# Layer 0 of a four-layer graph network on one NeuronCore: one strided sum per chunk in place of adding halves

## The chip, the core and the metric

The kernel runs on one core of one Trainium2 chip. The metric is the device time of one execution in microseconds; the time before is the median of three timed runs. One more execution was recorded by the hardware profiler. The engines are named as the profile names them: PE (TensorE's matmuls; PEld are its weight loads), DVE (VectorE), ACT (ScalarE), POOL (GpSimd) and SP (SyncE). In this kernel POOL issues the gathers and scatters through index lists (DMA_INDIRECT), and SP issues the plain DMAs.

## The reference

Four layers of message passing over the same graph: 3125 nodes with 128 features, 100000 edges sorted by destination. Each layer ends in a residual and a layer norm. Only layer 0 is touched by the change:

```python
z_bar = segment_sum(z[edge_type], dst) / max(deg, 1)
pre_self = h @ P1 + h @ P2 + z_bar @ P3
pre_edge = (h @ P1)[dst] + (h @ P2)[src] + (z @ P3)[edge_type]
logit_self, logit_edge = leaky(pre_self) @ y_w, leaky(pre_edge) @ y_w
alpha = softmax over a node's edges and its self edge        # 8 heads
t_self = h @ Wh + z_bar @ Wz
t_edge = (h @ Wh)[src] + (z @ Wz)[edge_type]
agg = segment_sum(alpha * t, dst)                            # 8 heads of 16
out = leaky(agg + residual_weight * h)                       # h itself where deg is 0
```

Layers 1 to 3 are a mean aggregation with a two-layer MLP, an attention with edge biases, and an attention with node and edge types.

## The kernel before

Nodes are ordered by degree and cut into 25 tiles of 128 (NT), one node per partition. A tile's edges stand in slots: tile t has CAP[t] of them, from 57 down to 21, 821 in all. Slots are worked in chunks of at most W = 8, so 114 chunks, 92 of them full. A loop for nodes of higher degree (`behind`, with `behind0` as its body) runs zero times on this input, so its gathers and sums are in the code and not in the trace.

For each chunk of layer 0, POOL gathers per slot one row of h_tab by source node into `hs` (264 numbers per slot: 128 for the logits, 128 for the message, 8 for the self logits). The edge's share by type comes in one of two ways:

- `gathered` (67 chunks, 45 of them full): POOL gathers per slot one row of z_tab into `zs` (328 numbers per slot: 264 that are added to hs, at L808, and 64 of z itself). The sum of the 64 over the slots is added to `za` (a part of the tile `az`), at L810.
- `multiplied` (47 chunks, all full): the edge types are made into one-hot matrices on VectorE (L834), and PE forms z transposed, `zT` (128 x 1024), from them. PE then forms the additions to hs (L849), which VectorE adds (L850). The sum of zT over the slots is kept in `zbT`.

Then PE transposes hs or multiplies it with the identity (L815, L843), VectorE adds the node's own term (L787), ACT applies a relu (L788), and PE forms the logits (L790). When all chunks of a tile are there, `masked` and `softmax` run, and `spread` (L872 to L874) multiplies each chunk's messages in hs by the weights in place, sums them over the slots, and adds the sum to `ac`, the other part of `az`.

`halved` makes these three kinds of sum: it adds the second half of the slots to the first (L796) until two are left, and adds those (L799). For 8 slots that is an add over 4 slots, one over 2 and one over 1. It works in place in hs and zs, and in `zh` for zT, whose first add is L853. The last reader of a chunk's `hs` is L874, and that of a chunk's `zs` is L810.

Buffers: hs has 8, so a gather into hs waits until the chunk eight places earlier has been spread. zs, zT and zh have 2 each.

Between the chunks a second job is interleaved step by step: `counts` builds, for layer 1, the matrix of edge counts from one-hot matrices (L562 to L639: c_oh, c_oha, c_ohb, c_ohs, c_ohd on VectorE, c_perm and c_ps on PE, c_sb on ACT, c_tab to DRAM by SP). At a tile's end the self edge, the norm and layer 1's first product follow (L929 to L988). For the next tile `prologue` gathers x (L772) one tile ahead.

The order of instructions on each engine is not the order of the source: a scheduler lays out each engine's queue ahead of the run, and each engine then works through its queue strictly in that order. So the same source lines can stand in another order when an instruction near them changes. Layers 2 and 3 do the weighted sum over slots in `weigh` (L696 to L701).

Of the kernel before, what the change touches and what calls it, by code (L numbers as in the profile page):

```python
# [8 lines left out]
F32 = mybir.dt.float32  # L9
# [4 lines left out]
OP = mybir.AluOpType  # L14
AX = mybir.AxisListType
# [3 lines left out]
P = 128  # L19
# [8 lines left out]
W = 8  # L28
D = 128
# [5 lines left out]
R = 64  # L35
HC = 2 * D + H
# [39 lines left out]
def tile_gnn(ctx, tc, a, out):  # L76
    nc = tc.nc
    V, A, G, T = nc.vector, nc.scalar, nc.gpsimd, nc.tensor
# [10 lines left out]
    def gather(dst, table, idx, **kw):  # L89
        return G.indirect_dma_start(out=dst, out_offset=None, in_=table, in_offset=indirect(idx), **kw)  # L90
# [394 lines left out]
    with tc.tile_pool(name="srcp", bufs=1) as sp, tc.tile_pool(name="srcq", bufs=2, space=PSUM) as ps:  # L485
# [28 lines left out]
        for o in range(0, NS, P):  # L514
            n = min(P, NS - o)
# [232 lines left out]
    with tc.tile_pool(name="l0", bufs=2) as wp, tc.tile_pool(name="l0s", bufs=1) as sp, \  # L748
# [14 lines left out]
        def sums_of(t):  # L763
            az = wp.tile([P, D + R], F32, name="az")
            nc.sync.dma_start(az, sums_at[t])
            return az[:, :D], az[:, D:], az
# [17 lines left out]
        def logits(pre, k, h1T, lg_ps):  # L784

            low = wp.tile([P, 4, P], F32, name="low")
            V.tensor_add(low[:, :k], pre[:, :k], h1T.unsqueeze(1).to_broadcast([P, k, P]))  # L787
            A.activation(low[:, :k], low[:, :k], AF.Relu)  # L788
            for s in range(k):
                T.matmul(lg_ps[:, s, :], low[:, s, :], yw8, start=True, stop=True)  # L790

        def halved(v, n, last=None):

            while n > 2:
                k = n // 2
                V.tensor_add(v[:, :k], v[:, :k], v[:, n - k:n])  # L796
                n -= k
            if n == 2:
                V.tensor_add(v[:, 0] if last is None else last, v[:, 0], v[:, 1])  # L799

        def gathered(h1T, idx, rl, n, za, lg_ps):

            hs = wp.tile([P, W, HC], F32, name="hs", bufs=8)
            zs = wp.tile([P, W, HC + R], F32, name="zs")
            for s in range(n):
                gather(hs[:, s, :], h_tab, idx(s))
                gather(zs[:, s, :], z_tab, rl[:, s:s + 1])
            V.tensor_add(hs[:, :n], hs[:, :n], zs[:, :n, :HC])  # L808
            halved(zs[:, :, HC:], n)
            V.tensor_add(za, za, zs[:, 0, HC:])  # L810
            for s0 in range(0, n, 4):
                k = min(4, n - s0)
                pre = ps.tile([P, 4, P], F32, name="pre")
                for s in range(k):
                    T.transpose(pre[:, s, :], hs[:, s0 + s, :D], ident)  # L815
                logits(pre, k, h1T, lg_ps[:, s0:s0 + k])
            return hs

        def multiplied(h1T, o, n, zbT, first, lg_ps):

            hs = wp.tile([P, W, HC], F32, name="hs", bufs=8)
            for s in range(n):
                gather(hs[:, s, :], h_tab, srcx[:, o + s:o + s + 1])
            rb = wp.tile([P, W * P], F16, name="rb")
            nc.sync.dma_start(rb[:, :n * P], rel_tab[o:o + n].rearrange("(o s) p -> o (s p)", o=1)
                              .to_broadcast([P, n * P]))
            zT = wp.tile([P, W * P], F32, name="zT")
            for s0 in range(0, n, 4):
                k = min(4, n - s0)
                cols = slice(s0 * P, (s0 + k) * P)  # L830
                oh = wp.tile([P, NK, 4 * P], BF16, name="oh")[:, :, :k * P]
                zps = ps1.tile([P, 4 * P], F32, name="zps")[:, :k * P]
                for i in range(NK):
                    V.tensor_scalar(oh[:, i], rb[:, cols], relid[:, i:i + 1], None, op0=OP.is_equal)  # L834
                    parts = [(zps, zq[:, i, :2 * R]), (zps[:R], zq[:, i, 2 * R:])]
                    for z, w in parts if i < NK - 1 else parts[::-1]:
                        whole = z is zps
                        T.matmul(z, w, oh[:, i], start=(whole and i == 0), stop=(whole and i == NK - 1))  # L838
                A.activation(zT[:, cols], zps, AF.Copy)
                pre = ps.tile([P, 4, P], F32, name="pre")  # L840
                T.matmul(pre[:, :k], zw[:, :D], zT[:, cols], start=True, stop=False)
                for s in range(k):
                    T.matmul(pre[:, s, :], hs[:, s0 + s, :D], ident, start=False, stop=(s == k - 1))  # L843
                logits(pre, k, h1T, lg_ps[:, s0:s0 + k])
            for s0 in range(0, n, 3):
                k = min(3, n - s0)
                t_ps = ps1.tile([P, 3, HC - D], F32, name="t_ps")
                for s in range(k):
                    T.matmul(t_ps[:, s, :], zT[:, (s0 + s) * P:(s0 + s + 1) * P], zw[:, D:], start=True, stop=True)  # L849
                V.tensor_add(hs[:, s0:s0 + k, D:], hs[:, s0:s0 + k, D:], t_ps[:, :k])  # L850
            assert n == W
            zh = wp.tile([P, W // 2, P], F32, name="zh")
            V.tensor_add(zh, zT.rearrange("z (s p) -> z s p", p=P)[:, :W // 2],  # L853
                         zT.rearrange("z (s p) -> z s p", p=P)[:, W // 2:])
            halved(zh, W // 2, zbT if first else None)
            if not first:
                V.tensor_add(zbT, zbT, zh[:, 0])
            return hs

        def masked(lg_ps, hss, n, mk):  # L860
# [7 lines left out]
        def spread(ac, hs, ex, n):  # L868

            val = hs[:, :n, D:2 * D]  # L870
            valh = val.rearrange("p s (h d) -> p s h d", h=H)
            V.tensor_tensor(valh, valh, ex.unsqueeze(3).to_broadcast([P, n, H, D // H]), op=OP.mult)  # L872
            halved(hs[:, :, D:2 * D], n)
            V.tensor_add(ac, ac, hs[:, 0, D:2 * D])  # L874

        def behind0(t, pl, mk, rl):
            _, _, h1T = prologue(t)
            ac, za, az = sums_of(t)
            lg_ps = ps1.tile([P, max(CAP), H], F32, name="lg")
            hs = gathered(h1T, lambda s: pl[:, s, 0:1], rl, W, za, lg_ps)  # L880
            lg = masked(lg_ps, [(0, W, hs)], W, mk)
            corr = softmax(wp, lg[:, :W], W, H, m[:, t, :], l[:, t, :])
            faded(ac, corr, H)
            spread(ac, hs, lg[:, :W], W)
            nc.sync.dma_start(sums_at[t], az)
# [13 lines left out]
        for t in range(NT):  # L899
            n = CAP[t]  # L900
            x, hw, h1T = ahead
            ac, za, _ = sums_of(t)
            lg_ps = ps1.tile([P, max(CAP), H], F32, name="lg")
            zbT = wp.tile([P, P], F32, name="zbT")
            hss = []
            mults = by_matmul(t)
            for s0, w in chunks(t):
                o = OFF[t] + s0
                if s0 + w == n and t + 1 < NT:

                    ahead = prologue(t + 1)
                if s0 in mults:
                    hs = multiplied(h1T, o, w, zbT, s0 == min(mults), lg_ps[:, s0:s0 + w])
                else:
                    hs = gathered(h1T, lambda s: srcx[:, o + s:o + s + 1], rel[:, o:o + w], w, za, lg_ps[:, s0:s0 + w])
                hss.append((s0, w, hs))

                done += n_steps * w / NS
                while done > 0:
                    next(steps, None)  # L920
                    done -= 1
# [3 lines left out]
            for s0, w, hs in hss:  # L925
                spread(ac, hs, lg[:, s0:s0 + w], w)
# [65 lines left out]
    with ExitStack() as ctx1, tc.tile_pool(name="l1", bufs=2) as wp, tc.tile_pool(name="l1s", bufs=1) as sp:  # L992
# [11 lines left out]
        rows = sp.tile([1, 1], I32, name="rows")  # L1004
# [120 lines left out]
    with tc.tile_pool(name="l2", bufs=2) as wp, tc.tile_pool(name="l2s", bufs=1) as sp, \  # L1125
# [100 lines left out]
        for t in range(NT):  # L1226
            qp = query(ps1, qb[:, t, :])
            for s0, s1, run in segments(t):
# [5 lines left out]
                n, o = s1 - s0, OFF[t] + s0  # L1234
# [46 lines left out]
    with tc.tile_pool(name="l3", bufs=2) as wp, tc.tile_pool(name="l3s", bufs=1) as sp, \  # L1281
# [28 lines left out]
        for t in range(NT):  # L1310
            n = CAP[t]
# [38 lines left out]
```

## Time and profile before

| | us |
|---|---|
| timed runs, median of 3 | 5862.23 (5854.55 to 5864.28) |
| profiled execution, its own time | 5814.11 |
| its span, first to last instruction | 5812.4 |
| DVE busy in the span | 3104.1 (53%), 6976 instructions |
| POOL busy in the span | 3074.3 (53%), 3136 instructions |
| PE busy in the span | 2236.2 (38%), 10027 instructions |
| ACT busy in the span | 934.1 (16%), 2437 instructions |
| layer 0's loop | about 200 to 3040 |
| layer 1 | about 3040 to 3240 |
| layers 2 and 3 | about 3240 to 5812 |

The profiled execution is shorter than the timed runs, and sums made from the trace are compared with its own time. The instructions of the lines that the change touches run from 240 to 3034 us after the span's start. The profile has three kinds of answers that matter here. Groups of instructions give, by line and shape, how often one ran, its busy time, its mean duration in ns, and how long the engine stood idle just before. Waits give how long an engine stood before instructions of one line, and which event came last before it went on. The timeline gives start, duration, engine, line and shape of instructions in order of time, with the idle time before in brackets. A named releaser is inferred: where it had long been done, it was another.

### The profile page before, as it was taken

The numbers are of one execution on the slowest core, as the hardware profiler recorded it, in microseconds if no ns is written. First come the engines' busy times: TensorE is split into PE (matmuls) and PEld (weight loads), VectorE is DVE, ScalarE is ACT, GpSimd is POOL, SyncE is SP. The second block draws the span as 40 slices with busy tenths as digits, with TensorE's granted clock in tenths as the row PEclk, the third lists the DMA queues.
The fourth block names the chain that finished last, engine by engine and source line by source line (L and its number), as shares of the span: only waits on it lengthen the run. The fifth ranks groups of instructions, "written<-read, shape, count | busy, mean of one in ns | idle before, by whom it ended". The sixth has DMA issues, their size and how long they took to land. (4 is left out here: it accounts for less than half of the span.)

```text
span 5812.4 us, 36204 instructions
## 1 busy us (share of the span) xinstructions
PE 2236.2 (38%) x10027; PEld 1363.8 (23%) x10027; DVE 3104.1 (53%) x6976; ACT 934.1 (16%) x2437; POOL 3074.3 (53%) x3136
## 2 busy tenths in 40 slices
PE   7165545555556556576658112222233200000000
PEld 5143333333334334344433001111111100000000
DVE  8354555554455446565652346565656455545555
ACT  1031222221222222222211001111111100000000
POOL 0555545545453544444640566566656366666664
PEclk9565556555665666566569555555555555555555
DMA  2423322322222222222335333333333233333332
GB/s 80 120 75 85 88 75 76 86 74 80 74 81 70 80 76 79 82 76 79 102 92 196 106 95 107 99 110 114 104 100 107 72 96 92 90 93 93 94 89 66
DMA packets 220239, 530.60 MB, mean 91 GB/s; under 512 B 65690, under 2 KB 112461, under 8 KB 215386
## 3 DMA queue, kind: packets, MB, share of 16 engines
q0 software_dynamic: 147968, 437.97, 26.6%
q1 hardware_dynamic: 72024, 89.90, 4.7%
q8 instruction: 87, 1.43, 0.1%
q14 instruction: 160, 1.30, 0.1%
HBM read 457.09 MB, written 70.63 MB: 91 GB/s over the span
## 5 line engine op out<-in xcount | busy, mean ns | idle before, releaser
L90 POOL DMA_INDIRECT hs<-h_tab,srcx x821 | 880.0, 1072 | 602.1 <-issue 448.7
L90 POOL DMA_INDIRECT kv<-kv_tab,pay_sb x821 | 782.1, 953 | 421.7 <-issue 239.5
L90 POOL DMA_INDIRECT kv<-ktv_tab,pay_sb x821 | 778.8, 949 | 332.3 <-issue 258.1
L90 POOL DMA_INDIRECT zs<-z_tab,rel x445 | 466.8, 1049 | 695.4 <-DVE az L810 303.3
L628 PE MATMUL c_ps<-c_ohs,c_ohd 128*128 128x128 bf16 x1300 | 334.3, 410 | 299.1 <-issue 110.3
L700 DVE TENSOR_REDUCE u<-msg 128x128 f32<-128x1024 f32 (+4 forms) x228 | 384.2, 1685 | 114.3 <-remote 69.6
L838 PE MATMUL zps<-oh,zq 128*128 128x512 bf16 x752 | 339.7, 516 | 88.3 <-DVE oh L834 80.1
L790 PE MATMUL lg<-yw,low 128*128 128x8 f32 x1642 | 306.4, 316 | 125.8 <-ACT low L788 81.6
L790 PEld LDWEIGHTS lg<-yw,low 128*128 128x128 f32 x1642 | 305.2, 276 | 162.8 <-ACT low L788 104.0
L628 PEld LDWEIGHTS <-c_ohd 128*128 128x128 bf16 x1300 | 187.2, 147 | 431.7 <-issue 256.2
L1295 DVE TENSOR_TENSOR qk<-kv,qp 128x1024 f32<-128x1024 f32 (+4 forms) x114 | 126.4, 1109 | 289.1 <-DMA kv<-ktv_tab,pay_sb 242.8
L623 DVE TENSOR_TENSOR c_ohs<-c_ends,c_up 128x1024 bf16<-128x1024 bf16 (+4 forms) x193 | 118.9, 616 | 248.0 <-remote 111.8
L696 DVE TENSOR_TENSOR msg<-kv,ex 128x1024 f32<-128x1024 f32 (+4 forms) x228 | 249.1, 1104 | 0.0
L604 ACT ACTIVATE c_oha<-c_oha,srclo 128x50 bf16<-128x50 bf16 (+2 forms) x821 | 201.5, 327 | 258.8 <-DVE c_oha L600 189.5
L850 DVE TENSOR_TENSOR hs<-hs,t_ps 128x408 f32<-128x408 f32 x141 | 74.5, 528 | 300.2 <-remote 193.0
L787 DVE TENSOR_TENSOR low<-pre,h1T 128x512 f32<-128x512 f32 (+1 forms) x215 | 141.3, 660 | 166.9 <-PE pre L843 76.1
L630 ACT ACTIVATE c_sb<-c_ps 128x512 bf16<-128x512 f32 (+1 forms) x175 | 96.5, 552 | 802.2 <-remote 363.0
L1143 DVE TENSOR_TENSOR qk<-kv,qp 128x1024 f32<-128x1024 f32 (+4 forms) x114 | 126.1, 1107 | 181.6 <-DMA kv<-kv_tab,pay_sb 173.1
L849 PE MATMUL t_ps<-zw,zT 128*128 128x136 f32 x752 | 153.7, 338 | 151.1 <-issue 105.1
L711 PE MATMUL tp<-ident,xk 128*128 128x128 f32 x100 | 42.3, 423 | 426.7 <-DVE xk L1211 88.6
L711 PE MATMUL tp<-ident,an 128*128 128x128 f32 x25 | 11.5, 461 | 434.5 <-DVE msg L696 174.3
L788 ACT ACTIVATE low<-low 128x512 f32<-128x512 f32 (+1 forms) x215 | 128.9, 606 | 274.7 <-DVE low L787 246.1
(394 smaller groups left out, 5252.7 us busy)
## 6 DMA issues: line engine op xcount, KB each, us to landing
c_tab<-c_sb SPq DMA_DIRECT2D x25, 768.0 KB
cs<-c_tab SPq DMA_DIRECT2D x6, 3200.0 KB
hs<-h_tab,srcx POOLq DMA_INDIRECT x821
kv<-kv_tab,pay_sb POOLq DMA_INDIRECT x821
kv<-ktv_tab,pay_sb POOLq DMA_INDIRECT x821
rb<-rel_tab SPq DMA_DIRECT2D x47, 256.0 KB
zs<-z_tab,rel POOLq DMA_INDIRECT x445
h_tab<-h SPq DMA_DIRECT2D x25, 132.0 KB
```

What stands on the lines that cost most here:

```text
L90: return G.indirect_dma_start(out=dst, out_offset=None, in_=table, in_offset=indirect(idx), **kw)
L604: A.activation(oha[:, s, 0, :], oha[:, s, 1, :], AF.Copy, scale=srclo[:, o:o + 1])
L628: T.matmul(cps[:, j * P:(j + 1) * P], ohd[:, :, nb * j + i], ohs[:, :, nb * j + i], start=(i == 0), stop=(i == nb - 1))
L696: V.tensor_tensor(msg[:, :n, :].rearrange("p s (h d) -> p s h d", h=heads), val.rearrange("p s (h d) -> p s h d", h=heads), ex.unsqueeze(3 ...
L700: V.tensor_reduce(u, msg[:, :n, :].rearrange("p s d -> p d s"), AX.X, OP.add)
L787: V.tensor_add(low[:, :k], pre[:, :k], h1T.unsqueeze(1).to_broadcast([P, k, P]))
L788: A.activation(low[:, :k], low[:, :k], AF.Relu)
L790: T.matmul(lg_ps[:, s, :], low[:, s, :], yw8, start=True, stop=True)
L838: T.matmul(z, w, oh[:, i], start=(whole and i == 0), stop=(whole and i == NK - 1))
L849: T.matmul(t_ps[:, s, :], zT[:, (s0 + s) * P:(s0 + s + 1) * P], zw[:, D:], start=True, stop=True)
L1143: V.tensor_mul(qk[:, :n], kv[:, :n, :D], qp.unsqueeze(1).to_broadcast([P, n, D]))
L1295: V.tensor_mul(qk[:, :n], kv[:, :n, :D], qp.unsqueeze(1).to_broadcast([P, n, D]))
```

## The change

`halved` goes, and `summed` takes its place: one tensor_reduce over the slots, read with a stride (the slot is the innermost index of the read). The reduction writes to a tile of its own: `zr` for zs, `hr` for hs, and zbT itself or `zh` for zT. zh shrinks from 4 x 128 to 128 numbers per partition. The adds into za, ac and zbT stay, and read the new tile. Everything else is as before, but the order in which the scheduler lays out layer 0's loop on the engines differs.

```diff
-        def halved(v, n, last=None):
-
-            while n > 2:
-                k = n // 2
-                V.tensor_add(v[:, :k], v[:, :k], v[:, n - k:n])
-                n -= k
-            if n == 2:
-                V.tensor_add(v[:, 0] if last is None else last, v[:, 0], v[:, 1])
+        def summed(to, rows):
+
+            V.tensor_reduce(to, rows.rearrange("p s d -> p d s"), AX.X, OP.add)
...
             V.tensor_add(hs[:, :n], hs[:, :n], zs[:, :n, :HC])
-            halved(zs[:, :, HC:], n)
-            V.tensor_add(za, za, zs[:, 0, HC:])
+            zr = wp.tile([P, R], F32, name="zr")
+            summed(zr, zs[:, :n, HC:])
+            V.tensor_add(za, za, zr)
...
-            zh = wp.tile([P, W // 2, P], F32, name="zh")
-            V.tensor_add(zh, zT.rearrange("z (s p) -> z s p", p=P)[:, :W // 2],
-                         zT.rearrange("z (s p) -> z s p", p=P)[:, W // 2:])
-            halved(zh, W // 2, zbT if first else None)
+            zh = zbT if first else wp.tile([P, P], F32, name="zh")
+            summed(zh, zT.rearrange("z (s p) -> z s p", p=P))
             if not first:
-                V.tensor_add(zbT, zbT, zh[:, 0])
+                V.tensor_add(zbT, zbT, zh)
...
-            halved(hs[:, :, D:2 * D], n)
-            V.tensor_add(ac, ac, hs[:, 0, D:2 * D])
+            hr = wp.tile([P, D], F32, name="hr")
+            summed(hr, val)
+            V.tensor_add(ac, ac, hr)
```

## The prediction

> **What bounds the kernel now.** I read the page first, then the busy time by stage, the waits of POOL, the forms of VectorE's instructions, and last the timeline around the longest POOL waits. The chain that ended last is no help: followed back, it stops at about 3250 us, and the changed lines run from 240 to 3034 us. So layer 0 is read from its own waits. Busy time by stage (columns: length, then PE, PEld, DVE, ACT, POOL busy with counts, PEclk, DMA share, GB/s); the first line is layer 0's loop:
>
> ```profile
> 200.00:3040.00 2840.00, 1634.99 (x7722) 1069.09 (x7722) 1511.84 (x3871) 673.92 (x1766) 1402.82 (x1340) 0.61 0.30 81
> ```
>
> No engine fills the 2840 us (DVE 53%, POOL 49%, PE 58%): the engines, each in its fixed order, wait for one another. The waits of POOL in that stretch (total us, times, longest) and the page's rows for the gathers:
>
> ```profile
> POOL zs L90 <- DVE az L810: 303.3, 17, 30.8
> POOL hs L90 <- PE c_perm L608: 97.8, 6, 22.9
> POOL zs L90 <- DVE c_bs L579: 81.1, 3, 40.7
> ```
>
> ```profile
> L90 POOL DMA_INDIRECT hs<-h_tab,srcx x821 | 880.0, 1072 | 602.1 <-issue 448.7
> L90 POOL DMA_INDIRECT kv<-kv_tab,pay_sb x821 | 782.1, 953 | 421.7 <-issue 239.5
> L90 POOL DMA_INDIRECT zs<-z_tab,rel x445 | 466.8, 1049 | 695.4 <-DVE az L810 303.3
> ```
>
> A gather costs POOL 0.95 us and 0.30 to the next, 1.25 in all. Going through the timeline of POOL, I find that each tile has one or two long stops. 30 stops before a zs gather (560 us) end 0.27 us after an L810 ends. 21 of the 24 hand-overs from tile to tile show a stop before an hs gather that ends 0.7 to 0.8 us after the first L874 of the tile's spread, whatever releaser is named. I call that L874 the gate. Between gates VectorE has a long idle piece (8 to 37 us) while POOL issues some 35 hs gathers, and then works at 85 to 95% up to the next gate. A tile's time is thus POOL's gathers after the gate, plus VectorE's in-order work from the last gather the tile needs to its own gate. Beside the gate at 1403 us, VectorE first, POOL second:
>
> ```profile
> 1403.19 0.28 DVE L874 TENSOR_TENSOR az<-az,hs 128x128 f32<-128x128 f32 x1
> 1403.39 1.21 DVE L872 TENSOR_TENSOR hs<-hs,lgs 128x1024 f32<-128x1024 f32 x1
> ...
> 1406.47 1.01 DVE L796 TENSOR_TENSOR hs<-hs 128x256 f32<-128x256 f32 x2
> 1407.40 0.28 DVE L799 TENSOR_TENSOR hs<-hs 128x128 f32<-128x128 f32 x1
> ...
> 1409.61 0.68 DVE L787 TENSOR_TENSOR low<-pre,h1T 128x512 f32<-128x512 f32 x1
> ```
>
> ```profile
> 1404.21 5.91 POOL L90 DMA_INDIRECT hs<-h_tab,srcx  x1 [24.35 <-PE t_ps L849]
> 1410.42 0.95 POOL L90 DMA_INDIRECT hs<-h_tab,srcx  x1 [0.30 <-issue]
> ```
>
> The reader is to see that the first gather past the gate takes 5.91 us, not 0.95, and ends just as L787 ends. L787 reads one input from PSUM; all that VectorE ran before it read two inputs from SBUF, back to back. Such first gathers took 6.97, 5.91, 5.91, 5.77, 5.45, 4.47, 4.12 us and less at other gates; over the 21 the excess above 0.95 is 46 us. Over all of layer 0's 1291 gathers the excess is about 150 us, and the 597 that overlap no VectorE instruction have none.
>
> **What the Trainium skill says.** "SBUF — State Buffer", section "Who interferes with whom": a VectorE instruction with two SBUF inputs shares a read interface with GpSimd and the later one waits; tensor_reduce never contends on trn2. The trace agrees on the stop above and in layers 2 and 3: kv gathers average 0.953 us beside strided sums (L700) and products whose second input is in PSUM. The page infers that descriptor generation is not held by tensor_tensor; this trace shows that it can be. "VectorE: DVE Perf Modes", "The perf-mode tier table", gives tensor_reduce and fp32 tensor_tensor one element a cycle. The trace agrees for a contiguous reduce (L1144, 1210 ns for 1024), not for a strided one:
>
> ```profile
> L700 DVE TENSOR_REDUCE u<-msg 128x128 f32<-128x1024 f32 x184 | 344.0, 1869 | 101.6 <-remote 64.7 <-issue 23.3 <-DVE msg L696 7.3
> L1144 DVE TENSOR_REDUCE lg<-qk 128x32 f32<-128x1024 f32 x92 | 111.3, 1210 | 15.4 <-remote 3.9 <-DVE mn L676 3.7 <-DVE an L1189 2.2
> L796 DVE TENSOR_TENSOR hs<-hs 128x512 f32<-128x512 f32 x92 | 61.5, 682 | 0.0
> L796 DVE TENSOR_TENSOR hs<-hs 128x256 f32<-128x256 f32 x101 | 40.4, 415 | 0.0
> L799 DVE TENSOR_TENSOR hs<-hs 128x128 f32<-128x128 f32 x110 | 29.6, 283 | 0.0
> ```
>
> **The change part by part.** Consecutive instructions start about 0.08 us before the one ahead ends (0.68 long, 0.60 apart), so a step costs its duration less 0.08.
>
> 1. VectorE's work. The spread of a full chunk did 0.60+0.335+0.20 = 1.14; the strided sum of the same 1024 elements is 1.79 (L700): +0.65, 92 times, +60. A multiplied chunk did 0.61+0.34+0.20 = 1.15 and gets 1.79: +0.64 x47 = +30. A full gathered chunk did 0.33+0.21+0.135 = 0.67; 512 elements strided cost 1.01-0.08 = 0.93 (L700 on 512): +0.26 x45 = +12. The 44 short sums add about 10 by L700's shorter forms. Together +112 us of VectorE on 1512, though 636 adds become 228 reductions. The strides here are 1056 and 1312 bytes against L700's 512, which no row shows. Bounds per full sum: 1.13 (contiguous rate) to about 2.3; I take 1.79, since L584, at other strides, has much the same rate (1.7 to 1.9 ns an element).
>
> 2. What of it lies on the path. In the changed kernel's instruction order most of a tile's spread stands behind the gate, in the stretch where VectorE later idles 8 to 37 us: hidden by POOL's 35 gathers of 1.25. If that cover were gone, the full 112 would show. From the last zs add of a tile (L808) to the gate, pricing each instruction in both orders by the trace's steps, VectorE has 569 us in all before and 545 after, and 248 waits on other engines against 288. The first chunk is gated earlier: two products and two interleaved chains of adds before (4.1 to 5.6 us), two products and one sum after (mostly 3.8). Measured, these stretches lasted 907 us in all. I take -24. Ahead of the last zs add, the first chunks' zT and zs sums of eleven early tiles are late by 0.64+0.26 each: +10.
>
> 3. The port. Past the gate stand one or two reductions of 1.79 us with a single SBUF input, so the waiting gather gets through within one product (1.2 us) at most. Of the 46 us I take -40, as each gather opens POOL's phase, which nothing covers. Bounds: 0 and -80, the latter if half of the excess elsewhere goes as well (by overlap, L796, L799 and L853 hold 42 of the 150).
>
> 4. zs released sooner. Its last reader was L810, four dependent steps after L808, interleaved with other work: 22 instructions later on average, 6 of them waiting on another engine. Now it is the sum itself, 7 instructions later with 2 waits. POOL's 560 us of zs stops will shrink a lot. But what follows such a stop is some 16 zs gathers and then the stop at the gate, 9 to 46 us long: POOL only comes earlier to a door that is still shut. Only in tile 0, where hs and zs gathers alternate and no gate follows, do I count it: the releases came 7.8 and 7.8 us after L808 and would come after 1.4 and 2.4: -10. Bounds: 0 and -150.
>
> 5. POOL's order. The gathers between a gate and the last one the next tile needs (zs tail or next x) are 811 before and 819 after over the tiles: +8 x 1.25 = +10. The x gather stands later in early tiles, the zs tail earlier and ahead of the scatter of x1. DMAs and their number are the same; SP's queue has a few swaps, which I cost at nothing: rb and u_tab are loaded ahead of their use. If one came late its tile would lose 2 to 3 us.
>
> Sum: +10 -24 -40 -10 +10 = -54; I forecast -50. The profiled execution has a span of 5812.4 and a time of 5814.1, 48 below the median of the timed runs (5862.2); taking the difference from the median gives 5812.
>
> **The rivals.** *Slower:* VectorE's added 112 us fall on the path. For it: VectorE is 85 to 95% busy in the second half of each tile, and in tiles 12 to 21 the idle pieces are only 8 to 20 us. It decides from the point where a tile's added 4.5 us stand before its gate and not behind it. With all of it on the path and the port's gain kept, +112-40 = +72; with half and half, +40: 5900. Against: the order puts most sums behind the gate. *No change:* the freed POOL time is lost at the next in-order wait (PE on the x gather, L985 on ACT), as with the zs stops: 5862. *Larger gain:* over the 30 stopped chunks 541 us lie between L808 and the release; priced without waits they are 248 before and 104 after, and with the same waits per step 104 x 541/248 = 227 after. Counted chunk by chunk, and never more than the stop, about 230 us of stops would go. If half of that reaches the path, 5862-50-115 = 5697. That the sums don't do what they say isn't open: every add of halves is gone from the order.
>
> **How the numbers follow.** Forecast 0.60, larger gain 0.10, no change 0.08, slower 0.22. The forecast's own range is 5770 to 5848, from the bounds of the port and of the strides. To hold 8 in 10 I reach down to 5735, part of the way to the larger gain, and up to 5895. A change within 0.2% (12 us) can't be told from none. Faster by more: 0.60+0.10 = 0.70; same 0.08; slower 0.22.
>
> **What would show it.** The strided sums near 1.8 us on hs; VectorE's busy time up by about 110 with fewer instructions. First gathers past the gates at 1 to 2 us; the mean hs gather from 1.07 towards 1.0. zs stops well under 560 us, gate stops longer. Wrong: gathers still stretched at the gates, sums of 2.2 us or more, or VectorE's long idle pieces gone.

## The result and the profile after

| | before | after |
|---|---|---|
| timed, median of 4 | 5858.39 us (5844.65 to 5864.28) | 5908.41 us (5905.92 to 5913.82) |
| ratio to before | 1 | 1.0093 [1.0077, 1.0109] |
| span of the profiled execution | 5812.4 | 5906.5 |
| DVE busy | 3104.1, 6976 instructions | 3229.3, 6568 instructions |
| POOL busy | 3074.3 | 3014.1 |

The changed kernel is slower by 0.9%, 50 us, where 50 us less was forecast. The two profiled executions differ by 94 us; the timed runs show that only some 50 of these belong to the change.

Busy time of layer 0's loop in the changed kernel (length, then PE, PEld, DVE, ACT, POOL busy with counts, PEclk, DMA share, GB/s):

```profile
200.00:3120.00 2920.00, 1625.21 (x7666) 1078.39 (x7722) 1632.56 (x3454) 673.32 (x1765) 1342.23 (x1340) 0.61 0.29 79
```

The last gate comes 78 us later. VectorE has 121 us more work in it, POOL 61 us less. The sums by shape in the changed kernel (count: shortest/median/longest duration in ns, first and last start in us, then the shapes):

```profile
L794 DVE TENSOR_REDUCE hr<-hs x114: 277/1978/2055, 417.3 to 3113.8; 128x128 f32<-128x1024 f32 x92, 128x128 f32<-128x128 f32 x4, 128x128 f32<-128x256 f32 x3, 128x128 f32<-128x896 f32 x3
L794 DVE TENSOR_REDUCE zr<-zs x67: 204/1064/1094, 293.5 to 3095.8; 128x64 f32<-128x512 f32 x45, 128x64 f32<-128x64 f32 x4, 128x64 f32<-128x128 f32 x3, 128x64 f32<-128x448 f32 x3
L794 DVE TENSOR_REDUCE zbT<-zT x25: 1881/1892/1935, 238.4 to 3085.6; 128x128 f32<-128x1024 f32 x25
L794 DVE TENSOR_REDUCE zh<-zT x22: 1874/1928/1972, 318.8 to 2797.4; 128x128 f32<-128x1024 f32 x22
```

A full hr sum takes 1.98 us, not the 1.87 that the forecast took from layer 2. POOL's gathers, from the page, answer to the rows of before:

```profile
L90 POOL DMA_INDIRECT hs<-h_tab,srcx x821 | 834.3, 1016 | 664.4 <-issue 554.8
...
L90 POOL DMA_INDIRECT zs<-z_tab,rel x445 | 447.3, 1005 | 648.3 <-DVE zr L794 392.7
```

The mean hs gather fell from 1.072 to 1.016 us, the mean zs gather from 1.049 to 1.005. At a gate, VectorE first and POOL second:

```profile
1420.34 2.36 DVE L866 TENSOR_TENSOR hs<-hs,lgs 128x1024 f32<-128x1024 f32 x2
1422.61 3.91 DVE L794 TENSOR_REDUCE hr<-hs 128x128 f32<-128x1024 f32 x2
1426.42 0.29 DVE L869 TENSOR_TENSOR az<-az,hr 128x128 f32<-128x128 f32 x1
```

```profile
1425.34 0.94 POOL L90 DMA_INDIRECT hs<-h_tab,srcx  x1 [42.56 <-PE pre L839]
1426.59 2.28 POOL L90 DMA_INDIRECT hs<-h_tab,srcx  x1 [0.30 <-issue]
```

The first gather past this gate takes 0.94 us; before the change it took 5.91 at this tile's gate. Over 21 gates the excess above 0.95 us went from 46.3 to 1.1 us. Some of it comes back in the gathers that follow (the second above takes 2.28 us beside a product): over the first four gathers past each gate the excess went from 59 to 25 us. For the reductions themselves that is what the Trainium skill's "SBUF — State Buffer", section "Who interferes with whom", says of tensor_reduce: it never contends with GpSimd. So the part of the forecast that was surest came true, and the kernel is slower all the same. Last, POOL's waits in the loop (total us, times, longest):

```profile
POOL zs L90 <- DVE zr L794: 392.7, 34, 30.6
...
POOL x L771 <- DVE y L969: 117.9, 13, 21.2
```

All stops before zs gathers together went from 569 to only 527 us (45 stops for 30), and stops before the memset of x, 31 us in the trace of before, came to 118 (one more, of 29 us, stands in both traces and is left out). I therefore began with the x buffer as the suspect. It was the wrong one.

### The profile page after: what moved, and what is told of

Same layout as the page of the kernel before. It is cut to its first block, busy times and chain, and to the rows that moved or that the text cites. A ratio compares the mean times of both kernels' runs of the same rounds, so it can differ in the third digit from the quotient of the medians.

```text
span 5906.5 us, 35692 instructions
## 1 busy us (share of the span) xinstructions
PE 2232.3 (38%) x9959; PEld 1375.3 (23%) x10027; DVE 3229.3 (55%) x6568; ACT 934.3 (16%) x2437; POOL 3014.1 (51%) x3136
## 5 line engine op out<-in xcount | busy, mean ns | idle before, releaser
L90 POOL DMA_INDIRECT hs<-h_tab,srcx x821 | 834.3, 1016 | 664.4 <-issue 554.8
L90 POOL DMA_INDIRECT zs<-z_tab,rel x445 | 447.3, 1005 | 648.3 <-DVE zr L794 392.7
L834 PE MATMUL zps<-oh,zq 128*128 128x512 bf16 (+1 forms) x696 | 319.9, 524 | 84.6 <-DVE oh L830 73.8
L630 ACT ACTIVATE c_sb<-c_ps 128x512 bf16<-128x512 f32 (+1 forms) x175 | 96.5, 551 | 746.6 <-PE c_ps L628 443.8
L794 DVE TENSOR_REDUCE hr<-hs 128x128 f32<-128x1024 f32 (+4 forms) x114 | 202.8, 1789 | 0.3 <-DVE hs L866 0.3
```

Source lines behind the costliest of these rows:

```text
L794: V.tensor_reduce(to, rows.rearrange("p s d -> p d s"), AX.X, OP.add)
```

## The experiments

A job is one batch of runs on one chip, with the kernel before among them. A ratio is to the kernel before in the same job; jobs are compared through these ratios alone, since the kernel before took 5853, 5815, 5144, 5809 and 5808 us in the five jobs of experiments. Each of the five ran on another chip, so what differs between jobs can be the chip as well as the occasion.

| run | edit | before, us | this, us | ratio [95%] |
|---|---|---|---|---|
| e1 | after, x with 3 buffers | 5853.0 | 5878.3 | 1.0060 [1.0038, 1.0082] |
| e2 | before, x with 3 buffers | 5853.0 | 5855.7 | 1.0001 [0.9988, 1.0015] |
| e3 | after, y's chain with priority | 5853.0 | 5900.2 | 1.0075 [1.0058, 1.0092] |
| e4 | after, every hr sum twice | 5853.0 | 6038.6 | 1.0319 [1.0303, 1.0334] |
| e5 | after, hr sums twice from the third chunk on | 5815.0 | 5886.8 | 1.0114 [1.0089, 1.0138] |
| e6, e14 | only the spread's sums strided | 5815.0, 5809.5 | 5781.9, 5773.0 | 0.9944 [0.9923, 0.9965], 0.9941 [0.9922, 0.9960] |
| e7 | only the zs sums strided | 5815.0 | 5871.9 | 1.0104 [1.0082, 1.0126] |
| e8 | only the zT sums strided | 5815.0 | 5825.8 | 1.0015 [1.0003, 1.0028] |
| e15 | spread and zT strided | 5809.5 | 5756.1 | 0.9904 [0.9887, 0.9921] |
| e18 | the same, x with 3 buffers | 5808.1 | 5749.2 | 0.9906 [0.9881, 0.9931] |
| e16 | after, zs held longer | 5808.1 | 5786.5 | 0.9958 [0.9941, 0.9975] |
| e13, e17 | after, again | 5809.5, 5808.1 | 5845.0, 5851.5 | 1.0062 [1.0046, 1.0077], 1.0073 [1.0054, 1.0093] |
| e9 | spread and zT strided | 5144.1 | 5069.0 | 0.9854 [0.9840, 0.9869] |
| e10 | after, zs held longer | 5144.1 | 5086.9 | 0.9885 [0.9870, 0.9899] |
| e11 | only the zs sums strided | 5144.1 | 5138.5 | 0.9983 [0.9977, 0.9990] |
| e12 | before, again | 5144.1 | 5144.6 | 1.0001 [0.9992, 1.0009] |

### Is it the x buffer, the order, or VectorE's work? (e1 to e4)

Three theories stood at the start. A: y (L969) is the last reader of x and now comes later, so x's two buffers are freed late. B: the order that the scheduler laid out is worse, whatever the sums cost. C: the 125 us of VectorE work lie on the path.

e1 and e2, in the changed kernel and in the one before:

```diff
-            x = wp.tile([P, D], F32, name="x")
+            x = wp.tile([P, D], F32, name="x", bufs=3)
```

> The changed kernel with three buffers for x instead of two, nothing else in the source; the layout then puts each x gather a tile earlier, ahead of the gate. Theory A (the late y keeps x's buffer, so POOL stops before the x memset and PE gets x late): the stops before the x memset, 118 us after the change, fall below 15, and the time falls to 5820 to 5870. Rival B (the loss is the layout's order of POOL alone): also a gain, since x is gathered earlier, but then the kernel before with the same edit gains about as much. Rival C (VectorE's 125 us of added work are on the path): 5895 to 5920, whatever happens to x.

> The kernel before with three buffers for x. Theory A: only 31 us of stops stood before the x memset here, so little is to be had: 5830 to 5860, and the changed kernel with the same edit comes within 20 us of it or below. Rival B: a gain of the same size as in the changed kernel, so the gap of 50 us stays. Rival C: 5850 to 5865, and the gap stays.

The third buffer made the scheduler fetch x a tile earlier still, and the stops fell only from 118 to 86 us. The ratio, 1.0060, is 0.0033 below the 1.0093 of the first pair, about 20 us; but the changed kernel as it was, which did not run in this job, gave 1.0062 and 1.0073 in later ones (e13, e17), so even this gain is not shown. Nothing came of the third buffer in the kernel before. The gap between the two kernels stays at 0.6%, so A explains at most a third.

e3 puts the self edge's chain ahead in the layout:

```diff
+            with tc.high_priority():
                 zaT_ps = ps1.tile([P, P], F32, name="tp", tag="misc")
...
                 V.scalar_tensor_tensor(y, x, has[:, 1:2], ac, op0=OP.mult, op1=OP.add)
```

> The changed kernel with the self edge, from the transpose of za to y (L924 to L969), given priority in the layout: the x gathers then stand 715 gathers behind the gates, summed over the tiles, as in the kernel before (802 in the changed kernel). The sums are unchanged. Theory A: y comes earlier, the stops before the x memset fall below 60 us, time 5840 to 5880. Rival B: the order is back and so is the time: 5850 to 5870, even if the x memset is still waited for. Rival C: 5895 or more.

The x gathers stand where they stood before the change, and the stops before x fell to 44 us, yet the ratio, 1.0075, lies among the 1.0062 to 1.0093 that the changed kernel itself gave in three jobs. A in this form and B in the form "x gathers are queued too late" fall.

e4 doubles the suspected cost:

```diff
             summed(hr, val)
             V.tensor_add(ac, ac, hr)
+            summed(hr, val)
```

> The changed kernel with each spread sum made a second time after the add into ac, into the same hr, where nothing reads it: some 200 us of VectorE work more, with POOL's order of x gathers the same (802). If work behind the gate is hidden by POOL's gathers, as the forecast had it: below +20 (5905 to 5930). Theory A: it pushes y back again, so x's buffer comes still later and about a third of it shows: 5950 to 6010, with the x memset stops above 150 us. Rival C: all of it shows, 6080 to 6120. Rival B: 5905 to 5930, as the order is the same.

VectorE's busy time rose by 192 us and the time by 130 to 150, by which ratio of the changed kernel one takes; no theory had that. The gate of tile 14, VectorE and then POOL, shows why:

```profile
2303.85 0.59 DVE L684 TENSOR_REDUCE sm<-lgs 128x8 f32<-128x248 f32 x1
...
2304.71 2.35 DVE L866 TENSOR_TENSOR hs<-hs,lgs 128x1024 f32<-128x1024 f32 x2
...
2308.53 3.93 DVE L794 TENSOR_REDUCE hr<-hs 128x128 f32<-128x1024 f32 x2
...
2314.03 1.98 DVE L794 TENSOR_REDUCE hr<-hs 128x128 f32<-128x1024 f32 x1
```

```profile
2316.76 0.94 POOL L90 DMA_INDIRECT hs<-h_tab,srcx  x1 [25.64 <-PE c_perm L608]
```

The scheduler interleaves the first two chunks, so that two products and three sums stand ahead of the first release. From the softmax's last sum to the release it took 11.6 us on average over 23 gates, against 6.3 over 22 in the changed kernel (and 7.5 over 21 before): some 5 us a gate, 128 us more in sum with the one gate more. That is about what the time rose by, so work ahead of the gate seems to cost nearly all of its length. The run left work behind the gate untested.

### Work behind the gate alone (e5)

```diff
-                spread(ac, hs, lg[:, s0:s0 + w], w)
+                spread(ac, hs, lg[:, s0:s0 + w], w, again=s0 >= 2 * W)
```

Theory H is the forecast's: behind the gate it is hidden, ahead of it everything counts. D says that VectorE's work counts anywhere.

> The changed kernel with the spread sum made a second time (nothing reads it) from a tile's third chunk on only: 64 of the 114 sums, some 115 us of VectorE more, all behind the gate; in the run that doubled all of them the stretch from the softmax to the gate grew by 128 us over the tiles, so that run did not tell work ahead of the gate from work behind it. Theory H (behind the gate POOL's gathers cover it, ahead of it everything counts): 5895 to 5925. Theory D (VectorE's work counts wherever it stands, at the 0.65 that the doubling of all gave): 5960 to 6000. Theory A (y is pushed back and x comes late): 5930 to 5960, with more stops before the x memset than 118 us.

VectorE's busy time rose by 99 us, the ratio from between 1.0062 and 1.0093 (the three jobs of the changed kernel) to 1.0114: 12 to 30 us. The stretch from the softmax to the release did not grow (130 us over the 25 tiles in both traces, up to the end of the releasing sum), so the added work did stand behind the gate. H is near, D is out. So C falls as well: 70 to 90% of this work is hidden.

### One part of the change at a time (e6 to e8, e14)

Each is the kernel before with one `halved` turned into the strided sum of the change:

```diff
-            halved(hs[:, :, D:2 * D], n)
-            V.tensor_add(ac, ac, hs[:, 0, D:2 * D])
+            hr = wp.tile([P, D], F32, name="hr")
+            summed(hr, val)
+            V.tensor_add(ac, ac, hr)
```

> The kernel before with the spread's sums alone turned into strided sums (114 of them); zs and zT still add halves. Theory H: the port's 45 us and some 25 us from the softmax to the gate are won, and nothing is paid: 5790 to 5830. Theory D: some 75 us of VectorE at 0.65 is +49, the port -45: 5840 to 5870. Theory A: the stops before the x memset rise to 80 to 120 us and eat the gain: 5850 to 5890.

> The kernel before with the sums over zs alone as strided sums (67 of them, 12 us of VectorE more). Theories H, D and A agree on little: 5845 to 5870. If the zs buffers' earlier release were worth something, POOL's stops before zs would fall well below 569 us and the time to 5800 or less; if it does harm (POOL comes ahead with zs gathers while others wait), 5875 or more.

> The kernel before with the sums over zT alone as strided sums (47 of them, 35 us of VectorE more), which stand among the logits and the adds into hs of the next tile. Theory H: those ahead of their tile's gate count, those before VectorE's idle piece don't: 5855 to 5880. Theory D: +23, 5870 to 5885. Theory A: they stand between the gate and y and push y back: stops before the x memset above 60 us, 5870 to 5900.

The spread's sums alone gain 0.6% (33 us), those over zT alone lose 0.15% (beside the spread's they gain, as e14 and e15 show in one job), and those over zs alone lose 1.0%, with some 20 us of VectorE's work in them (busy 3123.8 for 3104.1 us). The expectation had named such a loss, but only as one possibility. The trace of e7 is of no use for the place: its profiled execution, 5821 us, lay below all its timed ones (5852 to 5895). A second run of the spread alone confirmed the gain:

> The spread's sums alone, again (0.9944 in a job with pauses). Without pauses: the port's 45 us, and the stretch from softmax to gate, with nothing paid: 0.984 to 0.989. With pauses: 0.992 to 0.997. If zT's sums cost their 35 us of VectorE, it is faster than spread and zT together by 0.003 or more.

### Where the zs sums hurt: releasing zs or summing it? (e9 to e18)

Two theories. Z1: the sum into `zr` is zs's last reader, so zs is free sooner, and POOL's zs gathers run sooner; that costs. Z2: the strided sum itself stands badly. Spread plus zT (the changed kernel with `halved` put back for zs) tests that zs is the culprit. A version that sums into spare columns of zs keeps the strided sum and gives the release back to the add into za:

```diff
-            zs = wp.tile([P, W, HC + R], F32, name="zs")
+            zs = wp.tile([P, W, HC + 2 * R], F32, name="zs")
...
-            zr = wp.tile([P, R], F32, name="zr")
-            summed(zr, zs[:, :n, HC:])
+            zr = zs[:, 0, HC + R:]
+            summed(zr, zs[:, :n, HC:HC + R])
             V.tensor_add(za, za, zr)
```

> The changed kernel with the sums over zs back as adds of halves; the strided sums over hs and zT stay. If the parts add up (spread 0.9944, zT 1.0015, zs 1.0104 times the kernel before), the ratio to the kernel before is 0.994 to 0.999, so nearly all of the loss of the changed kernel goes. If the loss comes from the three together (VectorE's 125 us, of which 112 are still here), 1.004 to 1.010.

> The changed kernel with the sum over zs written into spare columns of zs itself, so that zs is released by the add into za, as before the change; the sum is the same strided one. Theory Z1 (the sum releases zs sooner, the layout and POOL then run zs gathers ahead of the x gather and of x1's scatter, and that costs): the ratio to the kernel before falls from 1.009 to 0.995 to 1.002. Theory Z2 (the strided sum itself, 0.93 us in one piece, stands badly among the logits): it stays at 1.007 to 1.011.

> The kernel before with only the sums over zs changed, once more, since its profiled execution (5821 us) lay below all its timed ones (5852 to 5895) and its trace may not show the loss. If the loss is real: ratio 1.007 to 1.013, and its trace, beside that of the kernel before in the same job, shows where; if it was chance: 0.998 to 1.004.

> The kernel before itself, for a trace and a time of the same job as the three others: ratio 0.998 to 1.002. It says how far two executions of one kernel lie apart.

In this job the kernel before took 5144 us, in its trace too (e12: span 5143.4). Here all versions gain, and the zs sums alone, 1.0% slower in the other job, are 0.2% faster. By its own expectation e11 would have called the loss chance; that it belongs to one kind of job is a reading made afterwards. What is absent in this job shows best on the eviction of c_ps (L630): the idle time of ACT before it, by what ended it, in the kernel before as first profiled, then in e12 (us, times):

```profile
its engine sat idle before it (us, times) until:
  remote: 363.0, 25
  PE c_ps L628: 354.0, 130
  issue: 82.5, 14
```

```profile
its engine sat idle before it (us, times) until:
  PE c_ps L628: 467.8, 172
```

The "remote" ones are waits that no instruction's end explains. Two normal rounds and two such ones in the kernel before, PE first, ACT second:

```profile
600.23 2.94 PE L628 MATMUL c_ps<-c_ohs,c_ohd 128*128 128x128 bf16 x12 [0.68 <-ACT c_sb L630]
603.86 2.94 PE L628 MATMUL c_ps<-c_ohs,c_ohd 128*128 128x128 bf16 x12 [0.68 <-ACT c_sb L630]
616.52 2.95 PE L628 MATMUL c_ps<-c_ohs,c_ohd 128*128 128x128 bf16 x12 [9.72 <-issue]
619.29 0.60 PE L815 MATMUL pre<-ident,hs 128*128 128x128 f32 x2
642.94 0.38 PE L790 MATMUL lg<-yw,low 128*128 128x8 f32 x1 [23.05 <-issue]
```

```profile
599.58 0.60 ACT L630 ACTIVATE c_sb<-c_ps 128x512 bf16<-128x512 f32 x1 [3.02 <-issue]
603.21 0.60 ACT L630 ACTIVATE c_sb<-c_ps 128x512 bf16<-128x512 f32 x1 [3.03 <-PE c_ps L628]
615.87 0.60 ACT L630 ACTIVATE c_sb<-c_ps 128x512 bf16<-128x512 f32 x1 [12.06 <-remote]
641.77 0.60 ACT L630 ACTIVATE c_sb<-c_ps 128x512 bf16<-128x512 f32 x1 [25.30 <-remote]
```

Twelve matmuls take 2.94 us, and the eviction at 603.21 starts when those of 600.23 are over. Those of 616.52 are over at 619.47, but ACT gets PE's semaphore only at 641.77, 22 us later, with VectorE idle as well, and POOL issuing gather after gather. I call this a pause of PE; since the profile models the ends of matmuls, it does not tell whether the matmul or only its signal was late. I followed every wait of ACT and VectorE on PE by the program's own semaphore counts to the matmul that ends it, and counted lags over 1.5 us with nothing else to wait for. In layer 0 of the kernel before that makes 67 pauses, 588 us, of which 496 lie inside runs of back-to-back gathers and 586 inside these or the 5.2 us after them (such stretches cover 63% and 74% of the loop). In e12 there is one, of 2.6 us, and in e9 and e10 none. The sums depend on how the lags are counted: with overlapping waits merged and each lag begun when the last other signal had come, the same trace gives 684 us in 85 pieces, e12 still none. Gathers alone don't make a pause: in e12 runs of them cover as much of the loop. What makes PE's signal late, and why one job was free of it, no run shows; as each job ran on a chip of its own, the chip may be the reason. "Who interferes with whom" in the Trainium skill's "SBUF — State Buffer" holds that DMA does not contend with compute engines and that PE waits on no one; it speaks of SBUF ports, which these traces can't separate, so no run here shows whether it holds for these pauses.

Theory P was then set up: the loss belongs to executions with pauses. The changed kernel had no run without them. Two more jobs were to close the comparison:

> The changed kernel again. Theory P (the loss belongs to executions in which PE's semaphores come late; without them the forecast's steps hold): in a job without such pauses, where the kernel before takes about 5144, the ratio is 0.985 to 0.992; in a job with them, where it takes 5800 or more, 1.006 to 1.012. Theory Z1 (the early release of zs costs by itself): without pauses the ratio is 0.992 to 1.000, clearly above the 0.9885 of the version that holds zs.

> Spread and zT, again (0.9854 in a job without pauses). With pauses: 0.994 to 0.999, if the parts add up as in the second job. Without: 0.984 to 0.987.

> The changed kernel with zs held until the add into za, again. In a job with PE's pauses (before at 5800 or more): if the early release of zs does the harm (theory Z1, through bursts of zs gathers during which PE pauses), 0.990 to 0.998 times the kernel before; if the strided zs sum itself does (Z2), 1.004 to 1.011 like the changed kernel beside it. Without pauses 0.987 to 0.990 as measured.

> The changed kernel, beside the version that holds zs. With pauses 1.005 to 1.011. Without pauses (before near 5144): theory P says 0.985 to 0.992, as no burst can hold PE up; Z1 by itself, without pauses, says 0.992 to 1.000.

Both jobs had the pauses. Without the strided zs sum the change gains 1.0% (0.994 to 0.999 was expected from the parts, so they don't simply add); with it and zs held it gains 0.4%; with zs released early it loses 0.7%. The release is thus worth 0.0115, some 67 us: Z1. It is not all: with zs held the ratio still lies 0.0054, some 30 us, above spread plus zT (0.9904; e18, with a third x buffer, gave 0.9906 in the same job as e16), and 0.0031 above it in the job without pauses. So about a third of what the zs part costs is left to Z2, the strided sum itself, or to the order laid out for it. Holding zs changes that order too, and the distance of the slots (1568 bytes for 1312, at the same 1.07 us a sum), so the release is not the only thing that differs. That the loss needs the pauses rests on e11 alone, one job on one chip. The two traces of one job, e13 and e15, agree in the stops before x's memset (86 and 90 us), which clears x for good. Their last gates are 82 us apart, and the pauses differ by 78 (622 and 544 us; by the merged count only by 48, 709 and 660). The difference thus points the right way, but does not fix how much of the loss is pauses. The end of one tile in e13 (changed kernel), VectorE, PE and POOL:

```profile
2338.54 2.36 DVE L803 TENSOR_TENSOR hs<-hs,zs 128x2112 f32<-128x2112 f32 x1
...
2346.61 1.06 DVE L794 TENSOR_REDUCE zr<-zs 128x64 f32<-128x512 f32 x1
...
2353.38 0.22 DVE L806 TENSOR_TENSOR az<-az,zr 128x64 f32<-128x64 f32 x1
2359.44 0.18 DVE L635 TENSOR_TENSOR outdeg<-outdeg,c_od 128x25 f32<-128x25 f32 x1 [5.85 <-PE t_ps L845]
...
2361.42 1.80 DVE L803 TENSOR_TENSOR hs<-hs,zs 128x1584 f32<-128x1584 f32 x1
```

```profile
2353.24 0.76 PE L634 MATMUL c_od<-onesb,c_sb 128*128 128x1 bf16 x25
```

```profile
2347.94 0.97 POOL L90 DMA_INDIRECT zs<-z_tab,rel  x1 [8.49 <-DVE u L982]
...
2356.75 0.95 POOL L90 DMA_INDIRECT zs<-z_tab,rel  x1 [0.30 <-issue]
2365.03 1.35 POOL L90 DMA_INDIRECT zs<-z_tab,rel  x1 [7.34 <-DVE zr L794]
```

The same place in e15 (adds of halves over zs; its lines L812, L800 to L803 and L814 are the add into hs, the halves and the add into za):

```profile
2305.41 2.35 DVE L812 TENSOR_TENSOR hs<-hs,zs 128x2112 f32<-128x2112 f32 x1
...
2314.03 0.42 DVE L800 TENSOR_TENSOR zs<-zs 128x256 f32<-128x256 f32 x1
...
2319.09 0.17 DVE L635 TENSOR_TENSOR outdeg<-outdeg,c_od 128x25 f32<-128x25 f32 x1
...
2321.23 0.21 DVE L803 TENSOR_TENSOR zs<-zs 128x64 f32<-128x64 f32 x1
...
2322.85 0.22 DVE L814 TENSOR_TENSOR az<-az,zs 128x64 f32<-128x64 f32 x1
...
2323.79 1.80 DVE L812 TENSOR_TENSOR hs<-hs,zs 128x1584 f32<-128x1584 f32 x1
```

```profile
2317.86 0.72 PE L634 MATMUL c_od<-onesb,c_sb 128*128 128x1 bf16 x23
```

```profile
2323.34 1.37 POOL L90 DMA_INDIRECT zs<-z_tab,rel  x1 [17.52 <-DVE az L814]
```

In e13 the sum ends at 2347.7 and releases zs at once; eight zs gathers run from 2347.9 to 2357.7. Meanwhile VectorE needs PE's c_od, over at 2354.0 by the records, and gets its signal at 2359.4: 5.85 us idle (the bracket names t_ps, since PE's records run on to 2358.5; by the program's counts the wait is for c_od), and everything up to the softmax is behind it in the queue. In e15 the last add on zs comes 8.8 us after the first half, the stop before zs is 17.5 us long, and nobody misses the gathers: VectorE takes c_od 0.5 us after PE is done. From the first chunk's add to the second's, 22.9 us there and 18.4 here. In this tile POOL's long stop was not lost time: PE, ACT and VectorE finished the tile in it. That the eight gathers delayed PE's signal is what the sequence suggests; no run shows it.

The last run added the third x buffer to spread plus zT, as a candidate:

> Strided sums over hs and zT, adds of halves over zs, and three buffers for x. With pauses: the third buffer took 32 us of stops before the x memset and 0.003 off the changed kernel, here 0.984 to 0.990 against 0.9904 without it. Without pauses there were no stops before the x memset, so 0.983 to 0.987, as without it.

It brings nothing, where 0.984 to 0.990 was expected: with x out of the path, that fits. Spread plus zT beats both kernels in both kinds of job, 0.9904 and 0.9854. Whether the changed kernel itself gains without pauses was not seen; the version that holds zs does, by 1.15%.

## Why the prediction was wrong

1. *VectorE's work.* Right, mis-sized by a tenth: 125 us for 112. At a stride of 1056 bytes 1024 elements cost 1.98 us, and at 1312 bytes 512 cost 1.06 (1.87 and 1.01 taken, before the overlap of 0.08). The tier table of the Trainium skill's "VectorE: DVE Perf Modes" gives one rate for all of them.
2. *What lies on the path.* Half right. e5 shows the cover behind the gate, and the stretch from softmax to gate shrank from 7.5 to 6.3 us a tile, some 25 us in all. That this is the size of the forecast's 24 is luck, for the 24 were those of a longer stretch, from a tile's last zs add to its gate: that one went from 908 to 799 us in the first two traces, and the zs sums alone shorten it as well (770 to 717 us over 24 tiles, e12 and e11) with hardly a gain in time, since VectorE comes later to the zs add (step 4). The cover was named wrongly. I read VectorE's idle pieces as waits for the data of POOL's gathers. In the traces with pauses the long ones mostly are PE's pauses (of 38 idle pieces over 8 us, 658 us in all, 449 us by the merged count); without pauses, in e12, 23 such pieces and 421 us remain. One case: the chunk whose last add VectorE reached at 2362 us in the kernel before had been gathered by 2230.
3. *The port.* Right: 45 us at the first gathers for the 40 taken, 34 over the first four past each gate, and over all 1291 gathers the excess went from some 150 to 87 us. What the traces show is that the gather is held; the prediction took it that its descriptors wait, but whether it is these or the reading of the index list, they don't tell.
4. *zs released sooner.* This is the step that failed. "POOL only comes earlier to a door that is still shut", -10 us, with bounds of 0 and -150: no loss was allowed for. The runs show a loss of some 67 us with the release (1.0073 against 0.9958), and some 30 more with the strided zs sum, which step 1 had at 12 and step 2 as good as hidden. The door was indeed shut: the stops at 21 gates grew from 313 to 381 us. But the zs stops, which were to "shrink a lot", went from 569 to 527, and what the earlier gathers do to VectorE was put at nothing. In e17 beside e16, of one job, POOL ends a tile's last zs gather sooner after the gate before (671 us for 776, summed over 24 tiles), but VectorE comes to the add that reads it later (1187 us after that for 1057), and from there to the gate takes 769 for 734: 61 us lost. Without pauses the same three sums are 672, 840 and 717 for the zs sums alone (e11) against 759, 703 and 770 before (e12): what POOL gains is waited away, and nothing is lost. That the early gathers bring on the late signals remains argued; the delay of VectorE is measured.
5. *POOL's order.* Without weight: spread plus zT has x gathers nearly as late in POOL's queue (778 gathers behind the gates, 802 in the changed kernel, 715 before) and is the fastest version.

Without step 4 the forecast's sum is -44 us, and spread plus zT, the change without its zs part, measured -53 with pauses and -75 without; with the reading of step 2 wrong, the nearness is in part luck. The rival "slower" had the sign and 5900 us, for another reason: it put the 112 us of VectorE on the path, which e5 refutes. "Larger gain" had looked at the right place, the zs stops, with the sign reversed.

## What to carry over

A buffer freed earlier shortened POOL's stops here and gained nothing; ask what will be running beside the work that starts earlier, who waits for its result, and allow a loss in the bounds. Before an idle piece is called hidden behind an engine, follow one wait in it to its producer's recorded end: a gap between that end and the signal is a cause of its own. And when a change has three parts, run each alone first; the smallest one, with a sixth of VectorE's added work, decided this case.

## What had not been expected of the hardware

- PE's semaphores came up to 36 us after the recorded end of the matmul that sets them, almost only beside runs of gathers or within 5.2 us after, 588 us in layer 0 of the kernel before; in one job of six (and on one chip) they did not, and the same kernel took 5144 us in place of 5808 to 5858. The cause is open. Layers 1 to 3 were shorter there too: 2533 us after the last gate, for 2781.
- Back-to-back VectorE adds with two SBUF inputs held a single gather up to 6.97 us; with reductions in their place the longest first gather was 1.41.
- A reduction over a stride of 1056 bytes ran at 1.93 ns an element, against 1.18 for the contiguous one of layer 2.
